# A graph network layer on one core: VectorE and ScalarE pick more of the gathers, and work is moved away from the first run and from the layer norm's wait

## The chip, the cores and the metric

The kernel runs on one NeuronCore of a Trainium2 chip. A core has five engines that run their own instruction queues: TensorE (PE) for matrix products into PSUM, VectorE (DVE) and ScalarE (ACT) for elementwise work, GpSimd (POOL) and SyncE (SP). [...] The metric is device time in microseconds (us). The kernel before takes 3654.95 us (median of 3 runs, 3654.35 to 3660.78).

## The reference

There are 12,500 nodes with 128 features (32 scalars, 32 vectors of three parts) and 412,500 edges, sorted by their end node `dst`. `src` is an edge's start node. For each edge

```python
e0 = feat0[edge_src]                       # features of the start node, 128 numbers with feat1
e1 = feat1[edge_src]
h = gelu(edge_scalar_attr @ W_mlp1 / sqrt(8))
h = gelu(h @ W_mlp2 / sqrt(64))            # 64 hidden numbers
w00, w01, w10, w11 = h @ Wp_00, h @ Wp_01, h @ Wp_10, h @ Wp_11   # 32 weights each
mid0 = concat(w00 * e0 * ea0, w11 * sum(e1 * ea1))
mid1 = concat(w01 * e0 * ea1, w10 * e1 * ea0)
```

The messages `mid0`, `mid1` are summed over the edges of each end node, multiplied by `W2`, mixed with a self term, and added to `x`. A layer norm over the 128 features of each node ends it (mean, variance, `(x - m) / sqrt(v + 1e-5)`). Everything is float32.

## The kernel before

**Runs and chunks.** The edges are cut into 806 *runs* of 512 (four columns, q = 0 to 3, of 128 edges, one edge to a partition). Four runs are a *chunk*; a run's place in it is `k = s % 4`. One Python loop writes out the instructions of all runs, s = 0 to 811, and sets the order by hand for PE, ACT, DVE and SP: what stands earlier in the loop stands earlier in its engine's queue. Each engine works through its queue in order and waits on semaphores for the others.

**Before the first run.** For 25 groups of 512 nodes `turn` transposes `x` into `xT` (features on partitions, one column of four bytes per node) and `features_of` multiplies it by the weights; DVE copies the product out of PSUM (L273) and ACT's queue stores it as the `table` in DRAM. In between stand loads of weights and edges and the index work of `load_indices`, all keyed by the number of the group in `extra`. Then `aid_load` (L125) loads the node numbers for the columns that are not gathered (below), and DVE turns them into byte addresses; `select`, `turn_rows(0)` and `features(0)` prepare run 0; `find_first` (L354) works out, on one partition, where each run's sums begin; and the sums are cleared.

**Getting the source rows.** A run needs 4 x 128 rows of node features in a tile `G` (20 buffers, so POOL may be up to 20 runs ahead). The first 18 runs gather raw rows of `x`, while the table is not there; PE multiplies them (`turn_rows`, `features`). From run 18 on they come from the table. There are four ways:

- POOL's indirect DMA, one per column (L197). Most columns go this way.
- SP moves the last column of every 14th run row by row (`aid`).
- DVE *picks* a column of some runs: node numbers are loaded into DVE's registers (L154), and one copy of a 128x1 column of `xT` for each edge fills a tile `GT` (L165). PE multiplies it by the weights (L173) and ACT puts the product into `G` (L174).
- ACT picks in the same way, with its own registers and copies (L167).

`COLS` says how many runs one pick is spread over: 5 on DVE, 6 on ACT. `pick_nodes(e, s)` splits the 128 copies into as many parts, in multiples of four, so that DVE makes 24 or 28 copies in a run and ACT 20 or 24. The picks are worked out ahead as `(first step, run at which it is multiplied, run that it serves)`.

**One run.** PE makes the edge weights into PSUM two runs at a time (`weights`, L532). DVE multiplies them with the rows (`messages`: L574, then L577 twice), makes the placing matrix from the run's end nodes (`placing`, L600, five buffers `PL`), and then loads registers and copies its picked columns. PE sums over edges with the same end node (`segments`, L591), ACT copies the sums (L594), and per chunk PE puts them to their places (`place`, L607) and DVE adds them into `acc` (`add`, L616, four of them at k = 2, at addresses loaded into registers at L611). At k = 3 DVE prepares the next chunk (`select`).

**Layer norm.** About every 33 runs a group of 512 nodes is complete. `norm` then calls, at k = 3, `moments` (PE adds the self term and the mixed sums, 20 products; ACT copies them to `y`, L641; DVE takes `bn_stats` from PSUM, L645, and `bn_aggr`, L646), moves the sums on to a new tile (ACT), and after every second group `normalise`: DVE adds epsilon (L653), ACT takes the root (L654, with a table load), DVE inverts and refines it (L655 to L660), ACT scales the rows (L668), SP stores them. All of that stands between one run and the next.

Of the kernel before, what the change touches and what calls it, by code (L numbers as in the profile page):

```python
# [8 lines left out]
F32 = mybir.dt.float32  # L9
I32 = mybir.dt.int32  # L10
# [10 lines left out]
P = 128  # L21
# [21 lines left out]
AID_FROM = 36  # L43
AID_LEAD = 16
STEPS = 12
COLS = {DVE: 5, ACT: 6}
COL_Q = {DVE: Q - 2, ACT: Q - 3}
COL_TURN = {DVE: (8, 0), ACT: (16, 1)}
LNB = 2
# [3 lines left out]
def gnn_kernel(ctx: ExitStack, tc: tile.TileContext, x, src, dst, ea4, ea8, w1_0, w1_1, wm1, wm2,  # L53
# [50 lines left out]
    G, GT, Y = {}, {}, {}  # L104
    aided = range(AID_FROM, NS - 1, AID)

    picked = {}
    for e, per in COLS.items():
        picked[e], (t, k) = [], COL_TURN[e]
        while True:  # L110
            at = t + per + 1
            at += (k - at) % CH
            if at + 2 >= NS - 1:
                break
            picked[e].append((t, at, at + 2))
            t += per
    pick_of = {(e, s): i for e, g in picked.items() for i, (_, _, s) in enumerate(g)}
    assert AID_FROM >= raw_runs and AID_LEAD < LEAD and P % ROWS == 0 and STEPS <= AID
    assert all(raw_runs <= g[0][2] and 0 < len(g) <= 2 * P for g in picked.values())
    assert 0 < len(aided) <= P  # L120

    aid_at = cst.tile([len(aided), P], I32)
# [2 lines left out]
    def aid_load():  # L125


        nc.sync.dma_start(aid_at, sub(src, AID_FROM * SB + (Q - 1) * P, [[AID * SB, len(aided)], [1, P]]))
        nc.vector.tensor_scalar(aid_at, aid_at, float(4 * P), None, op0=OP.mult)
        for e, g in picked.items():  # L130
            cycle = CH // math.gcd(CH, COLS[e])
            for h in range(0, len(g), P):
                part = g[h:h + P]
                rows = cst.tile([len(part), P], I32, name=f"pick{len(pick_rows)}")
                for i in range(min(cycle, len(part))):
                    n = len(part[i::cycle])
                    nc.sync.dma_start(rows[i::cycle], sub(src, part[i][2] * SB + COL_Q[e] * P,
                                                          [[cycle * COLS[e] * SB, n], [1, P]]))
                nc.vector.tensor_scalar(rows, rows, 4.0, float(x_at), op0=OP.mult, op1=OP.add)
                for i in range(len(part)):  # L140
                    pick_rows[e, h + i] = rows[i:i + 1]

    picking = {e: [] for e in picked}

    def pick_nodes(e, s):

        per = COLS[e]
        i, t = divmod(s - COL_TURN[e][0], per)
        if not 0 <= i < len(picked[e]):
            return  # L150
        if t == 0:
            GT[e, i] = wk.tile([P, P], F32, name=f"gt{list(picked).index(e)}", bufs=3)
        r0, r1 = (n * (P // 4) // per * 4 for n in (t, t + 1))
        _, r = nc.values_load_multi_w_load_instructions(  # L154
            pick_rows[e, i][:, r0:r1], engines=[e], min_val=x_at, max_val=x_at + 4 * (N - 1),
            skip_runtime_bounds_check_because="addresses of columns")
        for k in range(r1 - r0):
            at = r[k].with_bounds(guaranteed_mod_val=0, out_of_modulus=4)
            picking[e].append((GT[e, i][:, r0 + k:r0 + k + 1], x_bytes[:, bass.ds(at, 4)].bitcast(F32)))

    def pick(e, n):

# [7 lines left out]
    def picked_rows(e, i):  # L170

        pt = ps.tile([P, P], F32, name="h")
        nc.tensor.matmul(pt, GT.pop((e, i)), wf, start=True, stop=True)  # L173
        nc.scalar.activation(G[picked[e][i][2]][:, COL_Q[e], :], pt, AF.Copy)  # L174

    def aid(s, t):

# [107 lines left out]
    ones = cst.tile([P, 1], F32)  # L285
    spent = cst.tile([P, 1], F32)

    def line(dtype=F32):

        t = wk.tile([P, Q, 2, P], F32, name="M", bufs=3)  # L290
        return t.rearrange("p q a k -> p (q a k)").bitcast(dtype)[0:1, :NS]

    first_node = line(I32)

    w1r = cst.tile([P, HID], F32)
    block = cst.tile([P, 2 * Q], F32)
# [52 lines left out]
    assert all(len(bs) == 1 for c, bs in due.items() if c < NCH - 1)  # L349
    assert N - base[-1] + W <= ACC and ACC - GN <= GN  # L350
    first_at = cst.tile([1, NS], I32)
    assert NS <= Q * 2 * P

    def find_first():  # L354

        floor, strays = line(), line()
        nc.vector.memset(floor, 0.0)
        for c, bs in due.items():
            if (c + 1) * CH < NS:
                nc.vector.memset(floor[:, (c + 1) * CH:], float((bs[-1] + 1) * GN))  # L360
        nc.vector.tensor_tensor(floor, first_node, floor, op=OP.subtract)
        nc.vector.tensor_scalar(strays, floor, 0.0, float(ACC - W), op0=OP.max, op1=OP.min)
        nc.vector.tensor_copy(first_at, strays)
        nc.vector.tensor_tensor(strays, strays, floor, op=OP.not_equal)
        nc.vector.tensor_reduce(odd[0:1, 2 * NB:], strays, axis=mybir.AxisListType.X, op=OP.add)
# [28 lines left out]
        return off  # L394

    raws = {}
    scratch = wk.tile([P, 4, ACC], F32, name="acc")

    def rows_tile(part=None):

        if part is None:
# [219 lines left out]
    def moments(b, sums=None):  # L621
# [5 lines left out]
        j = len(pend)  # L627
        pend.append(b)
        pt = ps.tile([P, XB, P], F32, name="h")
        st = wk.tile([P, XB, 6], F32, name="bst")  # L630
        at = n0 - base[-1] if b in due[NCH - 1] else 0
        for t, k in tiles:
            nc.tensor.matmul(pt[:k, t, :], xT[:, n0 + t * P:n0 + t * P + k], ws, start=True, stop=sums is not None)
# [7 lines left out]
            nc.scalar.activation(Y["y"][:, j, :full, :], pt[:, :full, :], AF.Copy)  # L641
        if tail:
            nc.scalar.activation(Y["y"][:tail, j, full, :], pt[:tail, full, :], AF.Copy)
        for t, k in tiles:
            nc.vector.bn_stats(st[:k, t, :], pt[:k, t, :])  # L645
            nc.vector.bn_aggr(Y["v"][:k, j * XB + t, :], st[:k, t, :])  # L646

    def normalise(last=False):
        y, mv = Y["y"], Y["v"]
        n = len(pend) * XB  # L650
        a = wk.tile([P, 4, LNB * XB], F32, name="rs")
        v, r, u, m = a[:, 0, :n], a[:, 1, :n], a[:, 2, :n], a[:, 3, :n]
        nc.vector.tensor_scalar(v, mv[:, :n, 1], EPS, None, op0=OP.add)  # L653
        nc.scalar.activation(u, v, AF.Sqrt)  # L654
        nc.vector.reciprocal(r, u)  # L655

        nc.vector.tensor_tensor(u, r, r, op=OP.mult)
        nc.vector.scalar_tensor_tensor(u, v, -0.5, u, op0=OP.mult, op1=OP.mult)
        nc.vector.scalar_tensor_tensor(r, u, 1.5, r, op0=OP.add, op1=OP.mult)
        nc.vector.scalar_tensor_tensor(m, mv[:, :n, 0], -1.0, r, op0=OP.mult, op1=OP.mult)  # L660
        for j, b in enumerate(pend):
            for t, k in group(b)[4]:
                i = j * XB + t
                if last and t % 2:
                    nc.vector.tensor_scalar(y[:k, j, t, :], y[:k, j, t, :], r[:k, i:i + 1], m[:k, i:i + 1],
                                            op0=OP.mult, op1=OP.add)
                    continue
                nc.scalar.activation(y[:k, j, t, :], y[:k, j, t, :], AF.Identity,  # L668
                                     bias=m[:k, i:i + 1], scale=r[:k, i:i + 1])
            store_nodes(nc.sync, out, b, y[:, j])  # L670
        pend.clear()

    def norm(bs, last=False):
        for b in bs:
            moments(b)
            if not last:
                move_sums()
                new_sums()
            if len(pend) == LNB or b == 0:
                normalise(last)  # L680
        if last and pend:
            normalise(last)

    odd_f = cst.tile([1, 1], F32)
    odd_i = cst.tile([1, 1], I32)
# [9 lines left out]
    def general():  # L695
# [96 lines left out]
                                         out_offset=bass.IndirectOffsetOnAxis(ap=to, axis=0))  # L792
        for b in range(NG):
            moments(b, load_nodes(b, sums))
            if len(pend) == LNB:
                normalise()
        if pend:
            normalise()

    with tc.manual_schedule(engines={PE, ACT, DVE, SP}):  # L800
        load_raw_rows(nc.sync, 0, min(2, raw_runs))
        load_w1(nc.scalar)
        if raw_runs > 2:
            load_raw_rows(nc.scalar, 2, raw_runs)
        for s in range(min(LEAD - 2, raw_runs)):
            gather(s)
        nc.vector.tensor_scalar(ident, diag, 0.0, None, op0=OP.is_equal)
        for b in range(min(3, NG)):
            XT[b] = load_nodes(b)
        make_wf()  # L810
        clear()
        loads = list(weight_loads())
        extra = {2: lambda: load_edges(0), 3: lambda: load_attributes(0), NG // 2 - 2: lambda: turn_attributes(0), 4: lambda: load_raws(0), NG // 2: lambda: load_indices(0),
                 NG // 2 + 3: make_w1b, NG // 2 + 5: make_ws, NG - 6: lambda: radial(0), NG - 4: lambda: mlp1(0),
                 NG - 2: lambda: mlp2(0), NG - 1: make_wpost}
        for b in range(NG + 2):
            if b < NG:
                turn(b)
# [22 lines left out]
        select(0)  # L841
        turn_rows(0)
        features(0)
        find_first()
        new_sums()
        nc.vector.memset(A["next"], 0.0)
        A["now"] = A["next"]
        new_sums()
        clearing = [(0, a) for a in range(4)]
        pick_nodes(ACT, 0)  # L850
        for s in range(NCH * CH + CH):
            c, k = divmod(s, CH)
# [39 lines left out]
            if s < NS:  # L892
                messages(s)
                placing(s)
                pick_nodes(DVE, s)
                pick(DVE, P)
            if s + 1 < raw_runs:
                features(s + 1)
            if k == (1 if end else 2) and 0 < c <= NCH:
# [5 lines left out]
                clear_sums(clearing.pop(0)[1])  # L905
            if k == 3 and c + 1 < NCH:
                select(c + 1)
            if s == NS - 8:
                count_odd()

# [30 lines left out]
```

## Time and profile before

| | before |
|---|---|
| median of 3 runs | 3654.95 us |
| the profiled execution | 3654.6 us, span 3652.8 us |
| PE busy | 2618.5 us, 72% |
| DVE busy | 3077.8 us, 84% |
| ACT busy | 2391.7 us, 65% |
| POOL busy | 2736.6 us, 75% |
| granted PE clock | 0.83 |
| POOL gathers (L197) | 2,808 from the table, 72 from `x` |
| DVE picks (L165) | 20,224 copies |
| ACT picks (L167) | 16,640 copies |

The profile is of one execution. "Busy" counts an engine's own instructions; loads of registers, waits and the issuing of DMAs are not in it. In a line of a timeline the first number is the start in us from the start of the span, the second the duration (from first start to last end where several are merged, "x28"), then engine, line, operation and `out<-in`; in square brackets stands the idle time of that engine just before, and what ended it. In a line of a group stand busy time and mean ns of one, and behind the bar the engine's idle time ahead of these instructions with what ended most of it. "issue" is idle time in which the engine waited for nothing that the profile shows: for example its own queue's register loads. Neighbouring instructions of DVE and ACT overlap in the records, so a merged row, not the mean of one, gives the pace.

### The profile page before, as it was taken

To read this page: it belongs to the slowest core of one execution; us is meant where nothing else is said; L and a number is where in the kernel's file an instruction comes from. 1 tells how busy PE (TensorE), PEld (TensorE's weight loads), DVE (VectorE), ACT (ScalarE), POOL (GpSimd) and SP (SyncE) were. 2 spreads that over 40 slices of the span, in tenths; PEclk is the share of its full clock that TensorE was granted. 3 is DMA by queue.
4 is the path that set the end of the run, shared out by engine and by line. 5 is a ranking of instruction groups with operands and counts; after the bars stand their busy time and mean duration, and the time that the engine had idled before them with its cause. 6 is when DMAs were issued, how large, how long until landed. Compare 5 with 4: busy or idle time off the path is not lost.

```text
span 3652.8 us, 129429 instructions
## 1 busy us (share of the span) xinstructions
PE 2618.5 (72%) x29857; PEld 1938.9 (53%) x29857; DVE 3077.8 (84%) x25457; ACT 2391.7 (65%) x18614; POOL 2736.6 (75%) x2887
## 2 busy tenths in 40 slices
PE   5777777877677777677777677677677677677676
PEld 5555555655455555455555455555455555455554
DVE  3688898898898888887887888888888798798886
ACT  2377677677677667666766667666666676676673
POOL 7767777777777777777777777777777777777775
PEclk8989898788888878887788787887887787788877
DMA  9222332333332333322323322223222233233222
GB/s 207 57 57 67 63 63 64 63 63 71 63 63 65 63 63 70 63 62 63 63 59 68 67 60 63 67 60 69 64 62 63 63 63 63 65 63 62 59 64 48
DMA packets 578767, 243.66 MB, mean 67 GB/s; under 512 B 482186, under 2 KB 527072, under 8 KB 577984
## 3 DMA queue, kind: packets, MB, share of 16 engines
q0 software_dynamic: 92160, 188.93, 20.4%
q1 hardware_dynamic: 464542, 39.90, 8.9%
q10 hardware_dynamic: 21282, 6.47, 0.8%
q8 instruction: 238, 3.90, 0.5%
q14 instruction: 545, 4.46, 0.4%
HBM read 222.26 MB, written 12.80 MB: 64 GB/s over the span
## 4 chain that ended last, share of the span: by engine, by line
DVE 31%; issue 16%; POOL 16%; PE 10%; DMA 9%; SPq 7%; ACT 7%; DVEq 4%; ACTq 0%; POOLq 0%
POOL G L197 16%; DVE gt L165 13%; DMA G<-table,idx 8%; DVE M L577 7%; SPq L184 5%; ACT gt L167 3%; DVEq L154 3%; DVE M L574 3%; DVE acc L616 2%; DVE pl L600 2%; PE h L636 2%; PE seg L591 2%; PE w L532 2%; SPq L180 2%; DVE S L567 1%
## 5 line engine op out<-in xcount | busy, mean ns | idle before, releaser
L197 POOL DMA_INDIRECT G<-table,idx x2808 | 2667.1, 950 | 867.8 <-issue 737.2
L167 ACT ACTIVATE gt<-xT 128x1 f32 x16640 | 1664.4, 191 | 146.5 <-issue 144.9
L165 DVE COPY gt<-xT 128x1 f32 x20224 | 1301.6, 145 | 205.0 <-issue 194.2
L532 PE MATMUL w<-wpb,h 64*128 64x128 f32 x6448 | 730.9, 332 | 336.3 <-DVE M L577 334.0
L591 PE MATMUL seg<-M,S 128*32 128x128 f32 x12896 | 652.0, 322 | 419.1 <-DVE M L577 278.5
L532 PEld LDWEIGHTS w<-wpb,h 64*128 64x128 f32 x6448 | 587.5, 226 | 503.9 <-DVE M L577 388.9
L577 DVE TENSOR_TENSOR M<-w,G 128x384 f32<-128x384 f32 x1576 | 797.5, 548 | 0.0
L591 PEld LDWEIGHTS seg<-M,S 128*32 128x32 f32 x12896 | 343.6, 123 | 607.6 <-issue 152.1
L594 ACT ACTIVATE sg<-seg 128x256 f32<-128x256 f32 x403 | 150.9, 374 | 404.0 <-PE seg L591 391.5
L574 DVE TENSOR_TENSOR M<-w,G 128x256 f32<-128x256 f32 x788 | 323.4, 410 | 107.9 <-DMA G<-table,idx 93.7
L515 PE MATMUL h<-h,w2b 64*64 64x256 f32 x3232 | 319.2, 413 | 90.2 <-ACT h L504 87.4
L607 PE MATMUL m<-pl,sg 128*128 128x128 f32 x1612 | 333.0, 370 | 1.5 <-DVE acc L616 0.8
L607 PEld LDWEIGHTS m<-pl,sg 128*128 128x128 f32 x1612 | 282.1, 264 | 59.7 <-issue 57.6
L174 ACT ACTIVATE G<-h 128x128 f32<-128x128 f32 x288 | 79.3, 275 | 331.0 <-PE h L173 293.7
L500 PE MATMUL h<-eT,w1b 64*128 64x128 f32 x3232 | 280.3, 322 | 5.8 <-ACT eT L493 5.8
L500 PEld LDWEIGHTS h<-eT,w1b 64*128 64x128 f32 x3232 | 237.8, 222 | 56.1 <-issue 45.5
L515 PEld LDWEIGHTS h<-h,w2b 64*64 64x64 f32 x3232 | 146.6, 139 | 216.9 <-ACT h L504 177.4
L616 DVE TENSOR_TENSOR acc<-m,acc 128x128 f32 x806 | 234.2, 291 | 30.8 <-issue 2.7
L600 DVE TENSOR_SCALAR pl<-iota,colv 128x128 f32<-128x128 f32 x806 | 241.2, 299 | 5.1 <-PE m L607 5.1
L504 ACT ACTIVATE h<-h 128x512 f32<-128x512 f32 x404 | 215.7, 585 | 35.3 <-PE h L500 33.8
L520 ACT ACTIVATE h<-h 128x512 f32<-128x512 f32 x404 | 214.1, 580 | 19.8 <-PE h L515 14.0
L173 PE MATMUL h<-wf,gt 128*128 128x128 f32 x576 | 146.0, 345 | 14.4 <-ACT eT L493 10.2
(117 smaller groups left out, 1489.8 us busy)
## 6 DMA issues: line engine op xcount, KB each, us to landing
G<-table SPq DMA_DIRECT2D x7040, 0.5 KB
G<-table,idx POOLq DMA_INDIRECT x2808
e<-in_edge_attr SPq DMA_DIRECT2D x201, 64.0 KB
xt<-in_x SPq DMA_DIRECT2D x24, 256.0 KB
table<-ft ACTq DMA_DIRECT2D x24, 256.0 KB
xt<-in_edge_attr SPq DMA_DIRECT2D x24, 256.0 KB
out<-y SPq DMA_DIRECT2D x24, 256.0 KB
xt<-in_dst SPq DMA_DIRECT2D x5, 256.0 KB
```

The source lines that it names most:

```text
L165: nc.vector.tensor_copy(to, col)
L167: nc.scalar.activation(to, col, AF.Copy)
L197: nc.gpsimd.indirect_dma_start(out=G[s][:, q, :], out_offset=None, in_=x if s < raw_runs else table, in_offset=bass.IndirectOffsetOnAxis(a ...
L500: nc.tensor.matmul(p1[h][:, j // 2, j % 2, :], w1b[rows, j, :], eT[c][rows, :], start=True, stop=True)
L515: nc.tensor.matmul(p2[r][k * HID:(k + 1) * HID, h * n:(h + 1) * n], w2b[rows, :], H1[c][h][rows, k * n:(k + 1) * n], start=True, stop=True)
L532: nc.tensor.matmul(WP[i][:, q, :], H2[c][q % 2][rows, k, q // 2, :], wpb[rows, :], start=True, stop=True)
L574: nc.vector.tensor_tensor(m[:, :, :, :MUL], w[:, :, :2 * MUL].rearrange("p q (a u) -> p q a u", a=2), g[:, :, None, :MUL].to_broadcast([P, ...
L577: nc.vector.tensor_tensor(m[:, :, j, MUL:].rearrange("p q (i u) -> p q i u", i=3), w[:, :, None, (2 + j) * MUL:(3 + j) * MUL].to_broadcast ...
L591: nc.tensor.matmul(SEG[c][q * W:(q + 1) * W, r, :], own[:, r * Q + q, col:col + W], M[s][:, q, h, :], start=h == 0, stop=h == 1)
L600: nc.vector.tensor_scalar(PL[s], iota, colv[b][:, r:r + 1], None, op0=OP.is_equal)
L607: nc.tensor.matmul(pt[:, k].rearrange("p a n -> p (a n)"), SG[c][:, k, :], PL[s], start=True, stop=True)
L616: nc.vector.tensor_tensor(a, ST[c][:, k], a, op=OP.add)
```

## The change

- `COLS` becomes 4.5 and 5.5: nine runs give two picks on DVE and eleven give two on ACT. The copies of all picks are counted on as one stream (`done`), in multiples of four, so that DVE makes 28 copies in a run (32 in every ninth) and ACT 24 or 20; one step may end one pick and begin the next, and then loads registers for each.
- The picks' node numbers repeat their pattern every 8 picks instead of 4 or 2, so `aid_load` issues 32 loads instead of 12 for them on SP.
- The multiplication of these numbers into addresses (`addresses`), `find_first`, and the second tile of sums with its clearing are moved behind run 1. `find_first` sets its steps with 25 short memsets that do not overlap, instead of 24 that each run to the end of the row over the last. Its rows lie in the `scratch` tile and no longer in three buffers of `M`. The clearing of the first sums is moved among the groups before the first run (`extra` at group 13).
- The first transfer of raw indices, on SP, takes 3 runs instead of 2, and ACT's one run fewer.
- The layer norm's statistics are taken from the copied rows `y` in SBUF one run later (`norm_late` after that run's picks), with epsilon and root; the rest of `normalise` follows another run later. In the last chunk all stays together.

```diff
-COLS = {DVE: 5, ACT: 6}
+COLS = {DVE: 4.5, ACT: 5.5}
...
     for e, per in COLS.items():
-        picked[e], (t, k) = [], COL_TURN[e]
+        picked[e], (t0, k) = [], COL_TURN[e]
+        done = lambda t: int((t - t0) * (P // 4) / per) * 4
+        t = t0
         while True:
-            at = t + per + 1
+            while done(t) < (len(picked[e]) + 1) * P:
+                t += 1
+            at = t + 1
             at += (k - at) % CH
...
+        for t in range(t0, NS):
+            for i in range(done(t) // P, min(len(picked[e]), -(-done(t + 1) // P))):
+                steps_of.setdefault((e, t), []).append((i, max(0, done(t) - i * P), min(P, done(t + 1) - i * P)))
...
         nc.sync.dma_start(aid_at, sub(src, AID_FROM * SB + (Q - 1) * P, [[AID * SB, len(aided)], [1, P]]))
-        nc.vector.tensor_scalar(aid_at, aid_at, float(4 * P), None, op0=OP.mult)
         for e, g in picked.items():
-            cycle = CH // math.gcd(CH, COLS[e])
+            cycle = next(n for n in range(1, P) if n * COLS[e] % CH == 0)
...
-                nc.vector.tensor_scalar(rows, rows, 4.0, float(x_at), op0=OP.mult, op1=OP.add)
+                pick_tiles.append(rows)
...
+    def addresses():
+        nc.vector.tensor_scalar(aid_at, aid_at, float(4 * P), None, op0=OP.mult)
+        for rows in pick_tiles:
+            nc.vector.tensor_scalar(rows, rows, 4.0, float(x_at), op0=OP.mult, op1=OP.add)
...
+        for i, r0, r1 in steps_of.get((e, s), ()):
+            if r0 == 0:
+                GT[e, i] = wk.tile([P, P], F32, name=f"gt{list(picked).index(e)}", bufs=3)
+            _, r = nc.values_load_multi_w_load_instructions(
+                pick_rows[e, i][:, r0:r1], engines=[e], min_val=x_at, max_val=x_at + 4 * (N - 1),
+                skip_runtime_bounds_check_because="addresses of columns")
...
-        nc.vector.memset(floor, 0.0)
-        for c, bs in due.items():
-            if (c + 1) * CH < NS:
-                nc.vector.memset(floor[:, (c + 1) * CH:], float((bs[-1] + 1) * GN))
+        steps = [(0, 0)] + [((c + 1) * CH, (bs[-1] + 1) * GN) for c, bs in due.items() if (c + 1) * CH < NS]
+        for (r, n0), (z, _) in zip(steps, steps[1:] + [(NS, 0)]):
+            nc.vector.memset(floor[:, r:z], float(n0))
...
+    def stats(b, rows=None):
+        j = pend.index(b)
+        st = wk.tile([P, XB, 6], F32, name="bst")
+        for t, k in group(b)[4]:
+            nc.vector.bn_stats(st[:k, t, :], (Y["y"][:, j] if rows is None else rows)[:k, t, :])
             nc.vector.bn_aggr(Y["v"][:k, j * XB + t, :], st[:k, t, :])
+        return len(pend) == LNB or b == 0
...
+    def roots():
+        if "a" in Y and Y["of"] == pend:
+            return
+        Y["a"], Y["of"] = wk.tile([P, 4, LNB * XB], F32, name="rs"), list(pend)
+        v, r, u, m = parts()
+        nc.vector.tensor_scalar(v, Y["v"][:, :len(pend) * XB, 1], EPS, None, op0=OP.add)
+        nc.scalar.activation(u, v, AF.Sqrt)
...
+    late = []
     def norm(bs, last=False):
         for b in bs:
-            moments(b)
-            if not last:
+            rows = moments(b)
+            if last:
+                stats(b, rows)
+            else:
                 move_sums()
                 new_sums()
-            if len(pend) == LNB or b == 0:
-                normalise(last)
+                late.append(b)
...
+    def norm_late():
+        if late and late[0] == "rest":
+            late.pop(0)
+            normalise()
+        elif late and stats(late.pop(0)):
+            roots()
+            late.insert(0, "rest")
...
-        load_raw_rows(nc.sync, 0, min(2, raw_runs))
+        load_raw_rows(nc.sync, 0, min(3, raw_runs))
...
+                 NG // 2 + 1: lambda: nc.vector.memset(A["next"], 0.0)}
...
-        find_first()
-        new_sums()
-        nc.vector.memset(A["next"], 0.0)
         A["now"] = A["next"]
-        new_sums()
-        clearing = [(0, a) for a in range(4)]
+        clearing = []
...
                 pick_nodes(DVE, s)
                 pick(DVE, P)
+            norm_late()
             if s + 1 < raw_runs:
                 features(s + 1)
...
+            if s == 1:
+                addresses()
+                find_first()
+                new_sums()
+                clearing = [(0, a) for a in range(4)]
```

## The prediction

> **What bounds the kernel now.** I read the page's slices first, then POOL's groups and timeline, then DVE's groups, waits and timeline, and counted runs in the timelines.
>
> ```profile
> DVE  3688898898898888887887888888888798798886
> POOL 7767777777777777777777777777777777777775
> ```
>
> POOL's sevens are a full queue:
>
> ```profile
> 188.52 0.94 POOL L197 DMA_INDIRECT G<-table,idx  x1 [3.31 <-PE h L541]
> ...
> 198.72 0.95 POOL L197 DMA_INDIRECT G<-table,idx  x1 [5.51 <-ACT h L504]
> 199.97 0.94 POOL L197 DMA_INDIRECT G<-table,idx  x1 [0.30 <-issue]
> 201.21 0.94 POOL L197 DMA_INDIRECT G<-table,idx  x1 [0.30 <-issue]
> ```
>
> A gather starts every 1.25 us (1.255 on average). POOL's last waits of over half a microsecond end at 207 us; from 138 to 207 us they come to some 11 us, when all 20 `G` buffers are taken. 2,880 gathers fill POOL to 3630.8; 22 us of tail follow.
>
> DVE works in two regimes. Run 18's L574 starts at 196.6, run 230's at 1077.2: 880.6/212 = 4.154 us a run, and in that stretch DVE does not wait for a gather. From run 300 (1377.3) to 800 (3610.0) a run takes 4.465, which is POOL's rate: of a run's four gathers SP takes one in 14 runs, DVE one in 5 and ACT one in 6, so 3.562 are left, x 1.255 = 4.470. So DVE starts 97 us behind the gathers (run 18's last ends at 99.7), makes this up by about run 300, and then waits for them:
>
> ```profile
> L165 DVE COPY gt<-xT 128x1 f32 x20224 | 1301.6, 145 | 205.0 <-issue 194.2
> L574 DVE TENSOR_TENSOR M<-w,G 128x256 f32<-128x256 f32 x788 | 323.4, 410 | 107.9 <-DMA G<-table,idx 93.7 <-issue 5.7 <-PE h L173 2.5
> L645 DVE BATCH_NORM_STATS2 bst<-h 128x6 f32<-128x128 f32 x98 | 26.9, 275 | 84.5 <-ACT y L641 78.3 <-ACT y L643 4.4 <-issue 1.8
> ```
>
> 93.7 us of starvation is all the slack DVE has; 84.5 are lost before statistics. What a copy costs is seen in two neighbouring runs:
>
> ```profile
> 699.84 0.42 DVE L574 TENSOR_TENSOR M<-w,G 128x256 f32<-128x256 f32 x1
> 700.17 1.01 DVE L577 TENSOR_TENSOR M<-w,G 128x384 f32<-128x384 f32 x2
> 701.10 0.28 DVE L600 TENSOR_SCALAR pl<-iota,colv 128x128 f32<-128x128 f32 x1
> 701.48 1.79 DVE L165 COPY gt<-xT 128x1 f32 x28
> 703.19 0.41 DVE L574 TENSOR_TENSOR M<-w,G 128x256 f32<-128x256 f32 x1
> ...
> 704.65 1.54 DVE L165 COPY gt<-xT 128x1 f32 x24
> 706.12 0.41 DVE L574 TENSOR_TENSOR M<-w,G 128x256 f32<-128x256 f32 x1
> ```
>
> The run with 28 copies takes 3.35 us, that with 24 takes 2.93. A copy itself is 0.0625 (1.79 against 1.54 for four). The rest is the register load at L154, 1.665 us for 24 addresses and 1.901 for 28: DVE's queue loads while the multiplications run (1.5 us), and what is longer shows as "issue". A straight-line fit of the steps of runs 18 to 229 (norm runs and seven outliers left out) on place in chunk and copies gives 0.1215 us per copy: copy plus load, almost nothing hidden.
>
> **The change, part by part.** The sum is made for the profiled execution: 3654.6 us, span 3652.8, so 1.8 around it; the median shown is 3654.95.
>
> *More picks.* By the two schedules DVE picks 175 gathers for 158 and ACT 142 for 130: POOL has 2,851, 29 fewer, 36.4 us at 1.255. Its rate falls to 4 - 1/14 - 1/4.5 - 1/5.5 = 3.5245 gathers, 4.423 us a run. DVE has 28.44 copies a run for 25.6: 2.844 x 0.1215 = +0.346 us a run. The lower end is the copy alone, 0.178; the upper, copy plus a load of 0.066 an address (between L611's 4 and L154's 24), 0.365. I take the fit, since it was made in the regime that counts. ACT gets 1,536 copies at (1664.4 + 146.5)/16640 = 0.109: 167 us, hidden beside its waits for PE (391.5 at L594 alone); without them, 0.21 us a run.
>
> *Evened steps.* Where a step straddles two picks it loads twice: 875 loads on DVE for 790. The load of 4 addresses at L611 takes 0.347, so some 0.1 is fixed: 85 x 0.1 = 8.5 us, +0.011 a run. The Trainium skill ("DMA: Bandwidth & Descriptors", Latency and other measured facts) speaks against this part: it gives a register load a floor of about 600 ns, which would make the 85 loads an estimated 51 us; the 347 ns at L611 lies under that floor, so the row decides.
>
> *Late statistics.* The six norm runs between 18 and 230 take 6.7 us more than others at their place in the chunk. One is the wait at 719.12 (4.98 us for ACT's L641) and 1.7 us of statistics. Later, DVE has work between, and 1.72 of statistics, 0.07 of memset, half of 1.1 of normalising are left: 2.4, so -4.3 a norm, 24 norms in 806 runs, -0.128 a run. Queued behind the moved statistics on DVE are the next run's products; ACT's square root and scaling wait for them. The other end is 0: the wait comes back at another instruction. I take most of the gain: DVE reaches the statistics a run later, 4.3 us or more, and the mean wait is 3.4. Statistics of rows in SBUF no trace shows: between L646's 0.182 (SBUF) and L645's 0.275 (PSUM), at most 9 us in all; I take 0.275, the same instruction. The Trainium skill ("Perfetto Trace Analysis", Optimizing Scalar/DVE Operations) has DVE's access overhead 65 ns lower from SBUF than from PSUM; 98 of them would make an estimated 6 us, and no run here shows it.
> Three runs just after a normalisation (45, 109, 177) lose 6.3 us, as L600 waits for PE, and PE 6.9 us for ACT's L594, queued behind 3.2 us of L668: 0.030 a run. With scaling two runs later L594 is not behind it; I count -0.030, the other end being 0.
>
> Together: 4.154 + 0.346 + 0.011 - 0.128 - 0.030 = 4.353 us a run on DVE, under POOL's 4.423: the backlog shrinks by 0.07 a run, 54 us over the kernel, and is not used up. So DVE bounds nearly all of it.
>
> *Ahead of the first run.* Run 0's features are ready at 97.4 (L551), but its L574 starts at 107.85, after `find_first` (87.3 to 104.7) and a memset of 2.6. PE waits 8.32 us for it (L591), so I take 8.3 off: run 18 at 188.3. Ends: 0, if `find_first` costs the same at its new place, and 11. There it is five multiplications (1.0), 25 short memsets (about 0.08 by L626's 0.072, 2.0) and five operations of 4.1 us: 7 us from about 103 to 110, with run 3's features not due before 121.1 - 8.3 = 112.8. Without that cover it costs its 7 us. The memset of the sums goes beside the table's copies, where DVE waits 41.7 us at L273. The 20 more index loads cost SP 20 x 0.80 = 16 us (9.63 for 12): SP is free of them at 100 instead of 84, the addresses are wanted at 103; behind them stand the edges of chunk 4, wanted at about 130. On SP and ACT one raw run changes queue; POOL's 2.43 us wait at 15.9 goes, and is nothing while `G` buffers are full later.
>
> *Sum.* The last DVE copies come with run 795. 188.3 + 778 x 4.353 (3386.6) = 3574.9; runs 796 to 805 without copies, nine steps at PE's 2618/806 = 3.3: 30; the tail from run 805's L574 (3632.7) to the end, 20.1; around the span 1.8: **3627 us**, 0.8% faster.
>
> **The rivals.**
> *The floor:* DVE gains more than I count (under 4.335) and POOL stays the bound: 3654.6 - 28 x 1.255 - 8.3 = 3611; with all early waits and the 29th gather, 3604. For it: POOL was the bound before. Against: 0.018 a run decides.
> *No change:* 0.01 us a run is 7.8 us; at 4.38 to 4.40 the time is 3648 to 3663. That is DVE bound instead of POOL, for the same time.
> *Slower: the removed wait comes back.* The moments still need PE for 5.3 us at a stretch, and ACT stands in order behind them (L641 waits 113.6 for PE); its square root now waits for DVE, its scaling again one run later. If ACT's L594 comes late at the next place, DVE stops at L600. With half of 0.158 back a run costs 4.432 and the kernel 3689; with all, 3750. It decides from 0.045 a run, under a third. For it: PE's 6.9 us wait for L594; against: the five `PL` buffers and ACT's 65% load.
> *ACT as the bound:* (2391.7 + 146.5 + 167)/806 = 3.36 us a run, under 4.35; I give it nothing of its own.
>
> **How the numbers follow.** Forecast case 0.37 (own range 3612 to 3647), floor 0.14, no change 0.12, slower 0.37. About 0.2%, 7 us, is what a measurement can tell from no change. Faster 0.51, same 0.12, slower 0.37. The range runs from 3603 (the floor's low end) to 3700 (59% of the wait back); some 0.15 lies above.
>
> **What would show it.** Right: 2,851 gathers and 22,400 copies; L574 hardly waits for gathers after 1300 us; L645's 84.5 us down to 10; L165's "issue" up by about 140 (0.18 a run); run 18 near 188; 4.35 a run to 795. Wrong: new DVE waits at L600 or L574 for PE or ACT after norms; a run above 4.40; statistics that still wait; run 18 later than 193.

## The result, and the profile after

The kernel after takes **3669.23 us** (median of 6 runs, 3665.68 to 3673.53) against 3655.44 for the kernel before beside it (6 runs, 3654.10 to 3660.78): ratio 1.0035, 95% interval 1.0024 to 1.0045. It is slower by 0.35%, 42 us over the forecast and inside the range. The profiled execution took 3670.01 us, span 3668.2. Of the experiments below, only act_more and old_picks (e18) ran on chips on which the kernel before takes its usual 3656 to 3658 us; the others ran on chips on which it takes 5589 to 5678 us, at granted clocks of 0.63 to 0.68 for the kernels tried there, so they are told as ratios to the kernel before on the same chip.

In the profile after, the copies of L165 stand at L173, their register load at L162, the gathers at L205, the products at L580 and L583, the placing matrix at L606, `place` at L613, `add` at L622 with its register load at L617, the statistics at L656 and L657 (`y` from ACT's L646).

The slices of the page (busy tenths, 40 slices) after:

```profile
DVE  3699898999898998898888899888889998988997
...
POOL 7777777777777777777777677777777777777772
```

DVE has a nine in 19 slices, 8 of them in the later half; before it had 5, 2 of them there. POOL's last digit is a 2: it has issued its last gather at 3608.2 us, and DVE's product of run 805 begins at 3650.0, 42 us later. DVE is the bound from end to end.

DVE's groups after (busy, mean ns of one, then the idle time ahead of the group and what ended it):

```profile
L173 DVE COPY gt<-xT 128x1 f32 x22400 | 1434.7, 144 | 290.7 <-issue 265.8
...
L580 DVE TENSOR_TENSOR M<-w,G 128x256 f32<-128x256 f32 x788 | 321.3, 408 | 0.7 <-DMA G<-table,idx 0.2 <-issue 0.2 <-DMA G<-table 0.2
...
L656 DVE BATCH_NORM_STATS2 bst<-y 128x6 f32<-128x128 f32 x96 | 25.6, 267 | 10.5 <-ACT y L646 9.6 <-issue 0.9
```

The products wait 0.2 us for gathers in the whole kernel (93.7 before): the slack is used up. The statistics wait 9.6 us (78.3 before). Both were wanted, and yet the kernel is slower.

Where the time went, from the starts of the first product of runs 18 and 796 in the timelines and the ends of the spans, in us:

| | before | predicted | after | old_picks (e18) | act_more (e9) |
|---|---|---|---|---|---|
| start of run 18 | 196.6 | 188.3 | 182.8 | 184.8 | 183.8 |
| runs 18 to 796 | 3396.5 | 3386.6 | 3444.0 | 3401.3 | 3366.7 |
| run 796 to the end of the span | 59.7 | 50.1 | 41.4 | 59.6 | 58.6 |
| span | 3652.8 | 3625 | 3668.2 | 3645.7 | 3609.1 |

Two ends gained 13.8 and 18.3 us; the stretch between lost 47.5. Its step is 4.427 us a run (forecast 4.353), and it is that from the beginning:

| us a run | before | after | old_picks | act_more |
|---|---|---|---|---|
| runs 18 to 230 | 4.154 | 4.402 | 4.099 | 4.160 |
| runs 300 to 400 | 4.475 | 4.545 | 4.475 | 4.428 |
| runs 600 to 700 | 4.439 | 4.300 | 4.464 | 4.386 |
| runs 18 to 796 | 4.366 | 4.427 | 4.372 | 4.327 |

The kernel before ran its first 200 runs at 4.154, faster than POOL's 4.470, because DVE was behind the gathers. The kernel after takes 4.402 there, close to its own POOL rate of 4.423, so it never makes that time up.

### The profile page after: what moved, and what is told of

Its sections match the earlier page's. It is cut to its first block, busy times and chain, and to the rows that moved or that the text cites. A ratio compares the mean times of both kernels' runs of the same rounds, so it can differ in the third digit from the quotient of the medians.

```text
span 3668.2 us, 133560 instructions
## 1 busy us (share of the span) xinstructions
PE 2673.8 (73%) x29915; PEld 1979.4 (54%) x29915; DVE 3205.1 (87%) x27633; ACT 2527.9 (69%) x20179; POOL 2714.1 (74%) x2858
## 5 line engine op out<-in xcount | busy, mean ns | idle before, releaser
L205 POOL DMA_INDIRECT G<-table,idx x2779 | 2644.5, 952 | 870.8 <-issue 711.0
L175 ACT ACTIVATE gt<-xT 128x1 f32 x18176 | 1806.7, 191 | 172.0 <-issue 170.2
L173 DVE COPY gt<-xT 128x1 f32 x22400 | 1434.7, 144 | 290.7 <-issue 265.8
L597 PE MATMUL seg<-M,S 128*32 128x128 f32 x12896 | 640.6, 319 | 483.2 <-DVE M L583 283.9
L538 PE MATMUL w<-wpb,h 64*128 64x128 f32 x6448 | 757.6, 343 | 238.3 <-DVE M L583 236.1
L538 PEld LDWEIGHTS w<-wpb,h 64*128 64x128 f32 x6448 | 611.7, 235 | 419.0 <-DVE M L583 292.2
L583 DVE TENSOR_TENSOR M<-w,G 128x384 f32<-128x384 f32 x1576 | 796.0, 546 | 0.0
L521 PE MATMUL h<-h,w2b 64*64 64x256 f32 x3232 | 359.0, 455 | 114.5 <-ACT h L510 110.3
L600 ACT ACTIVATE sg<-seg 128x256 f32<-128x256 f32 x403 | 150.0, 372 | 268.6 <-PE seg L597 261.3
L613 PE MATMUL m<-pl,sg 128*128 128x128 f32 x1612 | 325.6, 364 | 1.7 <-DVE acc L622 1.0
L580 DVE TENSOR_TENSOR M<-w,G 128x256 f32<-128x256 f32 x788 | 321.3, 408 | 0.7 <-DMA G<-table,idx 0.2
L182 ACT ACTIVATE G<-h 128x128 f32<-128x128 f32 x317 | 87.0, 274 | 334.3 <-PE h L181 316.1
L613 PEld LDWEIGHTS m<-pl,sg 128*128 128x128 f32 x1612 | 274.8, 257 | 56.0 <-issue 53.9
L521 PEld LDWEIGHTS h<-h,w2b 64*64 64x64 f32 x3232 | 159.8, 151 | 257.3 <-ACT h L510 213.9
L622 DVE TENSOR_TENSOR acc<-m,acc 128x128 f32 x806 | 233.8, 290 | 31.2 <-issue 3.9
L606 DVE TENSOR_SCALAR pl<-iota,colv 128x128 f32<-128x128 f32 x806 | 238.8, 296 | 0.5 <-PE m L613 0.4
L510 ACT ACTIVATE h<-h 128x512 f32<-128x512 f32 x404 | 215.9, 585 | 20.1 <-PE h L506 18.7
L526 ACT ACTIVATE h<-h 128x512 f32<-128x512 f32 x404 | 214.7, 582 | 14.9 <-PE h L521 10.5
L181 PE MATMUL h<-wf,gt 128*128 128x128 f32 x634 | 155.9, 337 | 0.3
```

Of the source, the lines that this page charges most:

```text
L173: nc.vector.tensor_copy(to, col)
L175: nc.scalar.activation(to, col, AF.Copy)
L205: nc.gpsimd.indirect_dma_start(out=G[s][:, q, :], out_offset=None, in_=x if s < raw_runs else table, in_offset=bass.IndirectOffsetOnAxis(a ...
L521: nc.tensor.matmul(p2[r][k * HID:(k + 1) * HID, h * n:(h + 1) * n], w2b[rows, :], H1[c][h][rows, k * n:(k + 1) * n], start=True, stop=True)
L538: nc.tensor.matmul(WP[i][:, q, :], H2[c][q % 2][rows, k, q // 2, :], wpb[rows, :], start=True, stop=True)
L580: nc.vector.tensor_tensor(m[:, :, :, :MUL], w[:, :, :2 * MUL].rearrange("p q (a u) -> p q a u", a=2), g[:, :, None, :MUL].to_broadcast([P, ...
```

## The experiments

**act_more (e9): the changed kernel, VectorE back at one pick in 5 runs, ScalarE at one in 5.**

```diff
-COLS = {DVE: 4.5, ACT: 5.5}
+COLS = {DVE: 5, ACT: 5}
```

> The changed kernel with COLS 5 on VectorE (25.6 copies a run, as before) and 5 on ScalarE (25.6 for 21.3): the gathers come off POOL by way of ScalarE alone. Theory A (VectorE's queue bounds the changed kernel, ScalarE has time left): VectorE's step from run 18 to 230 is 4.05 us, POOL's rate 4 - 1/14 - 1/5 - 1/5 = 3.529 gathers x 1.255 = 4.428 us bounds the rest, and the time is 3605 to 3620 us. Rival (ScalarE's picks cost as much, as the chain runs through its queue too): 3655 us or more.

Measured: 3611.48 us (3610.99 to 3611.97) against 3656.41 (3651.28 to 3665.49), ratio 0.9874, interval 0.9827 to 0.9920. It beats both kernels. The page's slices and the DVE groups of this kernel:

```profile
DVE  3699898998898998888888889888898888888886
...
POOL 7777777777777777777777777777777777777775
```
```profile
L580 DVE TENSOR_TENSOR M<-w,G 128x256 f32<-128x256 f32 x788 | 322.3, 409 | 84.4 <-DMA G<-table,idx 68.2 <-issue 6.4 <-PE h L181 3.5
...
L656 DVE BATCH_NORM_STATS2 bst<-y 128x6 f32<-128x128 f32 x96 | 25.7, 268 | 39.7 <-ACT y L646 39.7
```

The products wait 68.2 us for gathers: POOL is the bound again, with 2,854 gathers for 2,880, and from run 300 on a run takes 4.43 us, which is 4 - 1/14 - 1/5 - 1/5 = 3.529 gathers at 1.255 (4.428). ACT's busy time is 2679.5 us, 74%: its 19,968 copies stay hidden. The early step, 4.160, missed its 4.05. The rows `y` come later from an ACT with more copies: the statistics wait 39.7 us instead of 9.6, the placing matrix 3.3 us between 184 and 900 us alone, and a layer norm costs DVE 9.0 us again (table below). So the rival "the removed wait comes back" exists, but here under POOL's bound.

**old_picks (e18, and e2, e8): the changed kernel with both old pick rates.**

```diff
-COLS = {DVE: 4.5, ACT: 5.5}
+COLS = {DVE: 5, ACT: 6}
```

> The changed kernel with VectorE's old pick count (5 of its 9-column runs' period as before), so the late statistics and the evened columns alone. Theory (extra picks cost 0.35 us a run, the late statistics save 3.5 us a norm of the 5.35 counted): on a chip where the kernel before takes about 3656 us, VectorE's step in runs 18 to 230 falls to 4.05 to 4.16 us a run and the time is 3638 to 3648 us, ratio 0.995 to 0.998. Rival (the moved statistics save nothing, the loads behind them eat it all): 3655 us or more. On a chip where the kernel before takes about 5590 us: ratio 0.975 again.

Measured: 3647.44 us (3646.56 to 3648.11, 6 runs) against 3658.45 (3656.48 to 3663.83, 7 runs), ratio 0.9965, interval 0.9951 to 0.9979. The step in runs 18 to 230 is 4.099. The theory's time, ratio and step all came, and the rival's 3655 us did not. (The expectation speaks of VectorE's picks; the edit sets both rates back.) With the late statistics and the lighter front alone the kernel is faster than before; only the pick rates lie between this kernel and the changed one, and they cost 3669.2 - 3647.4 = 22 us. That it is those on DVE follows from act_more, where more picks on ACT alone gained time. Its DVE group of the products shows who bounds it:

```profile
L580 DVE TENSOR_TENSOR M<-w,G 128x256 f32<-128x256 f32 x788 | 322.9, 410 | 155.7 <-DMA G<-table,idx 122.1 <-issue 14.6 <-PE m L613 6.7
```

122.1 us of waiting for gathers where the kernel before has 93.7: much of what the late statistics save goes into this wait. The last gather comes at 3622.4 instead of 3629.8, and this is the 7 us by which the span is shorter. It comes with the earlier start: POOL's waits of 14.3 us between 138 and 215 us (beside "issue") shrink to 3.3, and the first layer norm comes only at 280 us.

This kernel is also the one that prices the late statistics, since in runs 18 to 190 neither it nor the kernel before waits for gathers, and the copies are equal. The table has runs without norm or index work ("plain" runs, mean over the four places in the chunk), and what the eight runs from a norm on take beyond them. Its two rows on idle time add up the gaps between DVE's instructions in those eight runs, beyond the gaps of plain runs at the same places:

| runs 18 to 190, us | before | old_picks (e18) | after | act_more |
|---|---|---|---|---|
| plain run | 3.809 | 3.805 | 4.157 | 3.816 |
| a norm, mean of five | 9.14 | 5.40 | 5.33 | 9.04 |
| of it idle time of DVE | 5.16 | 1.56 | 1.57 | 4.94 |
| of that, ahead of the copies | 0.13 | 0.73 | 0.64 | 1.88 |
| step | 4.139 | 4.027 | 4.375 | 4.142 |

Late statistics save 3.7 us a norm, 0.112 a run. The picks add 0.352 to a plain run. DVE's waits between 184 and 900 us, which hold the same five norms (engine, what it waited for: us in total, times, longest), of before and of old_picks:

```profile
DVE gt L165 <- issue: 30.0, 69, 1.7
DVE bst L645 <- ACT y L641: 18.2, 4, 5.0
...
DVE bst L645 <- issue: 1.8, 1, 1.8
DVE pl L600 <- PE m L607: 1.5, 3, 0.8
DVE rs L655 <- ACT rs L654: 1.4, 3, 0.5
```
```profile
DVE gt L173 <- issue: 31.2, 73, 1.7
...
DVE bst L656 <- ACT y L646: 1.4, 1, 1.4
```

20.0 us at the statistics, 1.5 at the placing matrix and 1.4 at the reciprocal (which waits for ACT's root) become 1.4 in all: 21.5 us, 4.3 a norm. Of these 3.7 arrive in the step, since the idle time ahead of the copies grows by 0.6 a norm.

> The changed kernel with COLS back at 5 and 6: early start and late statistics alone. Theory A: VectorE's step from run 18 to 230 is 4.154 less 0.10, 4.05 us, POOL bounds the rest at 4.47 a run, and only the early waits of POOL (some 11 us) are won: 3643 us (3638 to 3648). Rival B: the late statistics cost time of their own: 3655 us or more, and a step of 4.15 or more.

> The kernel of e2 again (COLS at 5 and 6; early start and late statistics alone), on a chip where the kernel before takes its usual time. Theory A: step 4.05 from run 18 to 230, then POOL's 4.47: 3643 us (3638 to 3648). Rival B: 3655 us or more.

Measured: e2 0.9757 (0.9718 to 0.9797; 5445.43 us against 5589.27), e8 0.9747 (0.9689 to 0.9805; 5459.90 against 5590.65).

**changed (e16): the changed kernel itself, on a chip of the same kind as those two.**

> The changed kernel itself, as the measure for its variants on the same chip. On a chip where the kernel before takes 3655: 3669 us. Where it takes 5590, from the ratios there of statistics put back (0.995), no loads (0.967) and the old picks (0.975): theory A (late statistics gain on VectorE) wants it under 0.99; rival B (they gain nothing) 0.995 or more.

Measured: 5456.88 us against 5594.64, ratio 0.9754 (0.9712 to 0.9796). There the change is worth 2.5%, with the sign turned, and e2 and e8, whose intervals hold the same 0.9754, show no effect of its added picks there, neither way. No verdict on the usual chips is taken from these ratios.

**picks_only (e1): the kernel before with the new rates and the evened schedule alone** (`COLS`, `done`, `steps_of`, the 32 index loads, `pick_nodes`).

```diff
-COLS = {DVE: 5, ACT: 6}
+COLS = {DVE: 4.5, ACT: 5.5}
...
+        for i, r0, r1 in steps_of.get((e, s), ()):
```

> The kernel before with the new schedule of picks alone (175 and 142 picks; statistics, find_first and all else as before). Theory A (VectorE's own queue bounds the changed kernel; a run there has 2.84 more copies, each with its part of a register load, 0.35 us a run): VectorE's step from run 18 to 230 goes from 4.154 to about 4.50 us, above POOL's 4.42, so it is the bound throughout: 196.6 + 778 x 4.54 + some 43 = about 3770 us (3745 to 3795). Rival B (the late statistics cost the time, since ScalarE and TensorE wait longer elsewhere): the picks alone are then faster than the whole change, under 3660 us.

Measured: 5569.72 us against 5589.27, ratio 0.9962 (0.9932 to 0.9992). The microseconds expected can't be held against this chip. Alone, the picks gain a few tenths of a per cent there, with the interval's end close to 1.

**inline_stats (e3, e7, e12, e15): the changed kernel with statistics, root and scaling back at k = 3.** The edit also takes the statistics from PSUM again, as the kernel before does (`bst<-h` in its profile), though the expectation of e3 says that they still come from the copied rows.

```diff
-            if last:
-                stats(b, rows)
-            else:
+            full_up = stats(b, rows)
+            if not last:
                 move_sums()
                 new_sums()
-                late.append(b)
+                if full_up:
+                    normalise()
```

> The changed kernel with the layer norm's statistics, root and scaling back in place at k = 3 (statistics still from the copied rows). Theory A: each of 24 norms costs 3.5 us more on VectorE again, 0.10 us a run: 3669 + 80 = 3749 us (3725 to 3765), with about 85 us of waits ahead of the statistics. Rival B: 3669 us or less.

> The kernel of e3 again (statistics, root and scaling back at k = 3, picks and early start as changed), on a chip where the kernel before takes its usual time. Theory A: 3.5 us more for each of 24 norms, step 4.50, 3749 us (3725 to 3765). Rival B (the late statistics cost time elsewhere): 3669 us or less.

> The kernel of e3 again (statistics, root and scaling back at k = 3; picks and early start as changed). Theory A: 3.5 us more for each of 24 norms, step 4.50, 3749 us (3725 to 3765). Rival B (the late statistics cost time elsewhere): 3669 us or less.

> The kernel of e3 once more, alone in its call (statistics, root and scaling back at k = 3; picks and early start as changed). Theory A: on a chip where the kernel before takes 3655, 3.5 us more for each of 24 norms on VectorE, step 4.50 from run 18 to 230, 3749 us (3725 to 3765). Rival B (the late statistics cost as much elsewhere): 3669 us or less. Where the kernel before takes 5590: a ratio of 0.995, as in e3, e7 and e12.

Measured: ratios 0.9955 (0.9926 to 0.9984), 0.9952 (0.9919 to 0.9984), 0.9959 (0.9939 to 0.9980) and 0.9963 (0.9946 to 0.9981), on kernels before of 5589 to 5598 us. Against the changed kernel's 0.9754, the late statistics carry 2.0 points of its 2.5 there. That they save is shown on both kinds of chip; how much they save on the usual one comes from e18 alone, read in its trace.

**no_loads (e4, e6, e11, e13, e17): the changed kernel without DVE's register loads at L162.** It leaves out the node numbers: the copies take fixed columns of `xT`, so DVE's picked columns hold the rows of other nodes. The number of copies is unchanged.

```diff
+            if e == DVE:
+                for k in range(r1 - r0):
+                    j = (37 * (i + r0 + k)) % N
+                    picking[e].append((GT[e, i][:, r0 + k:r0 + k + 1], xT[:, j:j + 1]))
+                continue
             _, r = nc.values_load_multi_w_load_instructions(
```

> The changed kernel in which VectorE copies fixed columns and loads no addresses into its registers (so the picked rows are those of other nodes); number and shape of the copies stay. Theory A (the register load is longer than the products that run beside it and lies bare by 0.33 us a run): VectorE's step from run 18 to 230 falls from 4.40 to about 4.07 us, POOL bounds the rest at 4.42, and the time is 3604 to 3615 us. Rival C (the load is hidden; the idle time before the copies is the wait for other engines, or the copies' pace): the step stays at 4.35 to 4.40 and the time within 15 us of 3669.

> The kernel of e4 again (VectorE copies fixed columns and loads no addresses), on a chip where the kernel before takes its usual time. Theory A: VectorE's step from run 18 to 230 falls from 4.40 to about 4.07 us, POOL bounds the rest at 4.42 a run, 3604 to 3615 us. Rival C (load hidden): step 4.35 to 4.40, within 15 us of 3669.

> The kernel of e4 again (VectorE copies fixed columns and loads no addresses, so the picked rows are those of other nodes). Theory A: the step from run 18 to 230 falls from 4.40 to about 4.07 us, POOL bounds the rest at 4.42 a run, 3604 to 3615 us. Rival C (the load is hidden, the bare time is another wait): step 4.35 to 4.40, within 15 us of 3669.

> The kernel of e4 once more, alone (VectorE copies fixed columns and loads no addresses, so the picked rows are those of other nodes). Theory A (the register load is longer than the products beside it and lies bare by 0.33 us a run): the step from run 18 to 230 falls from 4.40 to about 4.07 us, POOL bounds the rest at 4.42 a run, 3604 to 3615 us. Rival C (the load is hidden, the bare time is another wait): step 4.35 to 4.40, within 15 us of 3669.

> The changed kernel with fixed columns and no loads of addresses on VectorE, beside the changed kernel itself. Theory A on a chip where the kernel before takes 3655: step 4.40 to 4.07 from run 18 to 230, 3604 to 3615 us; rival C (the loads are hidden): within 15 us of 3669. Where the kernel before takes 5590: 0.967 as in e4, against the changed kernel's own ratio.

Measured: 0.9668 (0.9632 to 0.9703), 0.9675 (0.9602 to 0.9748), one run of 5429.35 us against 5591.89, 0.9664 (0.9636 to 0.9693) and 0.9659 (0.9601 to 0.9716). The loads cost about 0.009 there (0.9754 - 0.966), some 50 us of 5594, though the intervals of e6 and e17 still touch that of e16. Most of the idle time ahead of the copies on these chips is something else: 1115.3 us of "issue" in e16 and still 1010.7 in e17, where nothing is loaded, against 265.8 for the changed kernel on a usual chip. What it is stays open, and it is why these ratios say little of the usual chips. On the usual chips the loads were not taken away; there the trace alone shows them lying bare.

**add_cover (e5, e10, e14): the changed kernel with the additions of k = 2 and the late statistics put between the load and its copies**, so that the load has more work to run beside.

```diff
                 pick_nodes(DVE, s)
-                pick(DVE, P)
             norm_late()
+            if k == 2 and not end and 0 < c <= NCH:
+                add(c - 1)
+            pick(DVE, P)
...
```

> The changed kernel with two places changed on VectorE's queue: the chunk's additions (k = 2) and the late statistics and scaling stand between a run's register load and its copies instead of behind the copies. Theory A2 (a semaphore wait ahead of a register load holds the queue, so that behind additions and statistics the next load starts with nothing left to run beside it: 0.53 us bare at k = 3 against 0.14 at k = 0, and some 0.8 a norm): about 0.35/4 + 0.025 = 0.11 us a run is won, the step from run 18 to 230 goes from 4.40 to 4.29, POOL's 4.42 bounds most of the rest, and the time is 3610 to 3625 us. Rival (the idle time before the copies comes from the load's length alone, wherever it stands): within 8 us of the changed kernel, 3669.

> The kernel of e5 again, now that the kernel before takes its usual time: on VectorE the additions (k = 2) and the late statistics and scaling stand between a run's register load and its copies. Theory A2 (a load behind additions or statistics lies bare, since the queue is empty beside it): the step from run 18 to 230 goes from 4.40 to 4.29, and the time is 3610 to 3625 us. Rival (the bare part comes from the load's length alone, wherever it stands): within 8 us of the changed kernel's 3669.

> The kernel of e5 once more, alone in its call: additions (k = 2), late statistics and scaling between a run's register load and its copies. Theory A2: on a chip where the kernel before takes 3655, the step from run 18 to 230 goes from 4.40 to 4.29 and the time to 3610 to 3625 us. Rival (the bare part of the load is the same wherever it stands): within 8 us of 3669. Where the kernel before takes 5590: a ratio of 0.97, as in e5 and e10.

Measured: 0.9726 (0.9662 to 0.9789), 0.9693 (0.9650 to 0.9735) and 0.9718 (0.9666 to 0.9769; this one against 5677.71 us). All three lie below the changed kernel's 0.9754, none is separated from it. Inconclusive: whether covering the load gives time back on the usual chips stays open.

## Why the prediction was wrong, point by point

**What bounds the kernel, and more picks: right.** DVE is the bound with 2,851 gathers and 22,400 copies. The added copies cost 0.352 us a run (plain runs 3.805 in old_picks, 4.157 after) where 0.346 + 0.011 were counted for picks and evened steps. DVE's copies between 184 and 900 us, in old_picks and after:

```profile
L173 DVE COPY gt<-xT 128x1 f32 x4495 | 289.1, 144 | 35.4 <-issue 31.2
```
```profile
L173 DVE COPY gt<-xT 128x1 f32 x4636 | 297.2, 144 | 54.9 <-issue 49.6
```

In fewer runs (164 against 176) the idle time ahead of the copies is 54.9 us, for 35.4: 0.33 a run, for 0.20. The load is bare, as the fit said. Over the whole kernel L173's "issue" rose by 72 us, not by 140, since the POOL-bound stretch before already had some.

**Late statistics: the first step that failed.** The prediction counted -4.3 us a norm for the wait and, as a second term, -1.05 (0.030 a run) for three stalls after a normalisation, together -0.158 a run. Measured: -3.7 a norm, -0.112 a run. Over 778 runs the two terms are short by 0.046 x 778 = 36 us.

The wait itself was sized nearly right: at the statistics and the reciprocal 21.4 us in the five norms become 1.4, so 4.0 of the 4.3 are gone, and 0.3 more at the placing matrix. The stalls were real too. In run 109 of the kernel before, the placing matrix waits 0.81 us for PE, and the register load, which stands behind it in DVE's queue, starts only then, at 579.4 us. It takes 1.65 us, and most of that lies bare ahead of the copies:

```profile
579.37 0.29 DVE L600 TENSOR_SCALAR pl<-iota,colv 128x128 f32<-128x128 f32 x1 [0.81 <-PE m L607]
581.12 1.55 DVE L165 COPY gt<-xT 128x1 f32 x24 [1.46 <-issue]
```

The step that failed is "With scaling two runs later L594 is not behind it; I count -0.030", and with it the choice to count the wait's gain as if next to nothing came in its place: those two terms hold no price for loads laid bare behind the moved work, which is 0.6 us a norm more idle time ahead of the copies, where the second term had less. In old_picks the bare loads of runs 45, 109 and 177 (0.88, 1.46 and 1.66 us before) shrink to 0.51, 0.04 and 0.15, as forecast. But the same stall comes at four other places: 1.62 us in run 77 and 1.06 in run 145, just behind moved statistics, and 1.30 in run 113 and 1.23 in run 181, four runs further on. Run 113 of old_picks, and the load of its copies (its duration three times over, then its start):

```profile
574.03 0.28 DVE L606 TENSOR_SCALAR pl<-iota,colv 128x128 f32<-128x128 f32 x1
575.62 1.55 DVE L173 COPY gt<-xT 128x1 f32 x24 [1.30 <-issue]
```
```profile
L162 DVEq TENSOR_LOAD <-pick x1: 1644/1644/1644, 573.9 to 573.9; - x1
```

PE's product (L613) for which the placing matrix has to wait ends at 573.85, 0.04 us ahead of the load, as in runs 109 and 177 before and in run 77 of old_picks. So the matrix itself loses nothing, but the load has no products left to hide behind. Why PE is late there is not shown; nine microseconds earlier it had waited 4.28 us for ACT's L600, which stood behind 3.19 us of the moved scaling.

The kernel after has the same: in the second run after each of the five norms, the idle time ahead of the copies lies 0.75 to 1.35 us above that of plain runs. One of them (start, duration, merged rows with their count, idle before):

```profile
584.65 0.18 DVE L657 BATCH_NORM_AGGREGATE mv<-bst 128x2 f32<-128x6 f32 x1
...
585.49 0.36 DVE L580 TENSOR_TENSOR M<-w,G 128x256 f32<-128x256 f32 x1
...
587.83 0.28 DVE L173 COPY gt<-xT 128x1 f32 x3 [0.83 <-issue]
```
```profile
L162 DVEq TENSOR_LOAD <-pick x1: 1900/1900/1900, 585.8 to 585.8; - x1
```

**The regime of the fit, the second step that failed: right where it was made, short later.** The sum took the step fitted in runs 18 to 230 for all 778 runs. Plain runs after take 4.157 us in runs 18 to 230, but 4.249 in 230 to 500 and 4.197 in 500 to 796: 0.092 x 270 + 0.040 x 296 = 37 us that no term held. The rise sits at k = 2 (+0.15) and k = 3 (+0.20) in runs 230 to 500, and there register loads are longer: of L617's in the stretch from 1400 to 2900 us, 70 take about 0.57 us and 11 take 0.35 (46 of 50 took 0.35 between 184 and 1066). At k = 3 the idle time ahead of the copies grows by as much as the run, from 0.59 to 0.78 us; at k = 2 all idle time grows by 0.08, so that part is only half accounted for. The kernel before has the same longer loads (78 of 84 at L611), but at POOL's rate they cost nothing: the forecast extended runs 18 to 230 over a stretch in which nothing could be read of DVE's own step.

These two terms, 36 and 37, less 4 for the picks and about 18 for the index work (about 10.5 us each time; it comes at 6 places in these 778 runs and at 2 in the 212 of the fit), make 51 of the 57 us by which the stretch is longer than forecast; 6 us stay unassigned.

**The price of statistics from SBUF.** `bn_stats` of rows in SBUF takes 267 ns, against 275 from PSUM: the forecast took 275. The Trainium skill ("Perfetto Trace Analysis", Optimizing Scalar/DVE Operations), cited in the forecast with 65 ns less from SBUF, is not borne out for this instruction: the row shows 8 ns less, and from the start of one statistic to that of the next it is 0.404 us for 0.411.

**Ahead of the first run: better than counted.** Run 18 starts at 182.8, not at 188.3; run 0's product starts at 94.0, 13.8 us earlier than before, where 8.3 were taken. `addresses` took 1.0 us, the 25 memsets 0.92 and not 2.0, and the 32 index loads on SP 20.8 us (0.65 each and not 0.80). In old_picks this part alone brings the last gather 7.4 us forward.

**The end: better than counted.** The nine steps from run 796 take 2.58 us each, not 3.3, and the rest 18.2 for 20.1.

**The rivals.** The slower case's sign came true, its mechanism in part and in another form: after, L656 waits 9.6 us, L606 0.5 and the products 0.7, but register loads behind a late `place` lie bare anew. Of the 0.158 a run, 0.046 came back, just the 0.045 from which this case was said to decide; most of the rest of the loss is the regime's. In act_more the wait itself came back. The floor of 3611 us came true there too, with the bound that the floor named: POOL at 3.529 gathers a run. It was the price of the picks on DVE that kept the changed kernel from it: its step of 4.427 lies 0.09 above the 4.335 from which this rival would have held.

## What to carry to other kernels

When work is moved from a bounding engine to another, compare the new step of the receiver with the average of the old kernel, start included, not with the old bound's rate: here DVE's 4.427 lies under POOL's 4.470 and still loses, because the old kernel ran 200 runs at 4.154. Give the work to the engine whose step has the slack: 26 more gathers picked on ScalarE, with none more on VectorE, made 3611 us; 17 more on VectorE and 12 on ScalarE made 3669. And a removed wait is not all gain: look at what stands behind the moved work in the queue. Here 4.3 us of waiting went for each norm and 3.7 arrived, because register loads lost their cover.

## What was not expected of the hardware

- Register loads on DVE grow by about 0.2 us in part of the program: at k = 3, 28 addresses take 1.9 us early and mostly 2.1 in runs 300 to 640, and the load of 4 addresses 0.57 for 0.35, in all four kernels traced on the usual chips. The cause is open. An estimate from the rise of the kernel after at k = 2 and k = 3 in runs 230 to 500, (0.15 + 0.20)/4, puts the cost at up to 0.09 us a run where the loads are bare.
- A load of addresses on DVE takes 0.35 us for 4, 1.64 for 24, 1.90 for 28 and 2.15 for 32 (medians): each further address costs about 0.06 us for loading, as much as its copy does. It keeps its place in the queue: where the instruction ahead of it has to wait, the load starts 0.04 us after that wait has ended (runs 109 and 177 before, 77 and 113 of old_picks).
